# Two layers of cross attention on one core: projections cut from 384 to 320 columns, and two reciprocals written to SBUF

## The chip, the cores and the metric

The kernel runs on one core of a Trainium2 chip. The metric is the device time of one execution in microseconds (us), from three runs. A core has a matrix engine (PE, whose weight loads are listed apart as PEld), a vector engine (DVE), a scalar engine (ACT), a general engine (POOL), and a sync engine (SP), which here does nothing but issue DMAs. Each takes its instructions in the order of its own queue and waits on semaphores of the others.

## The reference

Two attention layers follow one another on `x` (16 samples, 256 queries, 320 channels) with a context of 16 x 256 tokens x 512 channels. Each layer has 20 heads of 16 channels. Cut to its core, layer 0 is:

```python
text, ip = ctx[:, :77], ctx[:, 77:]
q, k, v = hs @ Wq, text @ Wk, text @ Wv            # 320 columns each
text_out = softmax(q_h k_h^T * scale) v_h           # per head
text_probs = softmax(q k^T * scale)                 # over all 320 channels
sem = (text_probs @ text) @ ip^T * scale
ip_out = softmax(q_h (ip @ Wk_ip)_h^T * scale + 0.5 * sem) * mask @ (ip @ Wv_ip)_h
out = (text_out + ip_out) @ Wout + bout + hs
```

Layer 1 has 252 text tokens and 4 image tokens; its `sem` is a cosine between the attended text of a head and the image tokens. All numbers are 32-bit floats, and the result has to be close to a 32-bit one.

## The kernel before, in words

**High and low parts.** A matrix product is made on PE from operands that are split into a high part, which PE takes without loss, and a low part, the rest. `halves(hi, lo, src)` makes them: ACT copies `src` into `hi` (L147), DVE or POOL subtracts (L148). A full product is high x high + high x low + low x high, that is three matmuls for each 128 rows of the contraction (`prod`, L205).

**Tiles of columns.** Channels of q and k stand as (d, h), 16 x 24 with 4 heads of padding, so 384 columns, three tiles m = 0, 1, 2 of 128 (`CP = 384`, `HP = 24`). The output weights and the residual are padded to 384 by repeating the last 64 of the 320 columns. So 64 of the 384 columns, a sixth, carry nothing that is needed. The places:

- `keys0` and `keys_first` (layer 0, a pair of samples at a time) and `keys1` (layer 1, a sample at a time): for each m, 12 matmuls `prod` of 4 row tiles x 3 terms. Layer 0 does it twice, with 192 columns for the text keys and 360 for the image keys; layer 1 with 252. `keys_out` sends high, high, low to the DRAM buffer `kd`.
- `project` (L542): for each m, 8 matmuls of 256 columns. `queries` uses it with `wq` (L550, L551 make the high and low parts `q`, and three DMAs write them to the DRAM buffer `qd`); `finish` uses it with `wo`, and DVE adds bias and residual (L768).
- `semantic0` (L588) multiplies all three tiles of q with all three of the text keys `kb`, 192 columns of the two parts side by side.

**Stacks and slots.** The heads' operands are read back from `qd` and `kd` in another layout, four heads of a group at a time, into a ring of `qs` and `ks` (`stacks0`, `stacks1`, four slots ahead of use: `LEAD = 4`). There are 80 slots in each layer, five to a sample. A slot of layer 0 makes scores (L666), their maxima (DVE L667, L668), transposes the maxima on PE (L674), sends them into `qs` by four small DMAs of the ACT queue, makes the turned scores (L690), their exponentials (ACT L693), a product with the image factor on POOL (L696) and the sums over values (L723). A slot of layer 1 does the like (L814, L816, L834, L808, L828, L868) and the norm of the attended text (L846, L847, L856, L857, L878).

**Order.** PE's order is written out by the program (`slot0`, `slot1`, and tasks with due times in slots, `task(...)`, which `fill` steps through between the parts of a slot). During the first slots (`begin`) all engines follow the program. After that only PE's queue is pinned; the queues of DVE, ACT, POOL and SP are ordered by the compiler's scheduler. Every DMA is issued from SP (L82), but for the maxima's, which ACT issues (L678, L838).

**PSUM.** Eight banks: scores two, T two, P one, X three. All projections, keys, semantics and norms rotate through the three X banks. `settle0` and `settle1` normalize a slot's result: DVE transposes the bank P into `nt` (L734, L913), writes the reciprocals back into that bank (L737, L738, L922) and multiplies by them (L740, L923).

Of the kernel before, what the change touches and what calls it, by code (L numbers as in the profile page):

```python
# [8 lines left out]
F32 = mybir.dt.float32  # L9
# [7 lines left out]
B = 16  # L17
S = 256
# [15 lines left out]
XROW = 48  # L34

# [13 lines left out]
def xattn2(  # L49
# [47 lines left out]
    words, slots = {"ctb": 1024, "cta": 1024, "raw": 512, "rawc": 512, "kb": 1152, "si": 256, "sp": 128, "wC": 2 * 4 * (H * D + NIP), "mt": S, "mx": 2, "tmp": (NG + 1) * 48, "kst": 4 * S, "rs": 2 * S, "P": 4 * S}, {}  # L97
# [21 lines left out]
    kd = [dram.tile([B // 2, 3, CP, 2, S], F32, name="kd0"), dram.tile([B, 3, CP, 1, S], F32, name="kd1")]  # L119
# [25 lines left out]
    def halves(hi, lo, src, eng=nc.vector, loaded=False):  # L145
        order = queued if loaded else lambda inst: inst
        order(nc.scalar.copy(hi, src))  # L147
        order(eng.tensor_sub(lo, src, f(hi)))  # L148
# [21 lines left out]
    def weights(w_d, tag, half=None, wait=0, raw="raw"):  # L170

        rows, n = w_d.shape
        kt = rows // 128
        w = buf(tag, [128, 2, kt, n], FR)
        yield from in_turn([(w_d[k * 128 : (k + 1) * 128], w[:, 0, k], w[:, 1, k]) for k in range(kt)], wait, raw)
        if half is not None:
            nc.vector.tensor_scalar_mul(w[:, 1, 2], f(w[:, 1, 2]), half)
        return lambda s, k, m=slice(None): w[:, s, k, m]

    def weights_by_column(w_d, wait=0, raw="raw"):  # L180
# [4 lines left out]
        return lambda s, k, m: parts[m.start // 128][:, s, k]  # L185

# [21 lines left out]

    def context(b, n, wait=0):
# [9 lines left out]
        if n == 2:  # L219
# [7 lines left out]
    wkt = buf("wA", [128, 2, 4, CP], FR)  # L227
    wk0 = lambda s, k, m=slice(None): wkt[:, s, k, m]
    wqt = buf("wE", [128, 2, 3, CP], FR)
    wkit = [buf("wB", [128, 2, 4, 128], FR, bufs=SIZES["WB"]) for m in range(3)]  # L230
    wki0 = lambda s, k, m: wkit[m.start // 128][:, s, k]
    rows = lambda w, k: w[k * 128 : (k + 1) * 128]
# [3 lines left out]
            (*ctx0[k], ("rawc", "raw")[k // 2]), (rows(wk0_d, k), wkt[:, 0, k], wkt[:, 1, k], "P"))],  # L236
# [4 lines left out]
    wki_src = wki0_d.rearrange("(k p) n -> p k n", p=128)  # L241
    all_halves(
        [(rows(wq0_d, k), wqt[:, 0, k], wqt[:, 1, k], ("rawc", "raw")[k // 2]) for k in range(3)]
        + [(wki_src[:, :, m * 128 : (m + 1) * 128], w[:, 0], w[:, 1], "P") for m, w in enumerate(wkit)],
        RINGS,
    )
    nc.vector.tensor_scalar_mul(wqt[:, 1, 2], f(wqt[:, 1, 2]), tmask[:, 3:4])
# [7 lines left out]
    wq, wo = [lambda s, k, m=slice(None): wqt[:, s, k, m]], []  # L255
# [27 lines left out]
    hsn = const_tile([128, 3, 8, 2, 16], "hsn")  # L283

# [4 lines left out]
    def keys_out(d, m, kst, b=slice(None)):  # L289

        rows = slice(m * 128, (m + 1) * 128)
        for r, s in ((slice(0, 2), 0), (slice(2, 3), 1)):
            src = kst[:, s, b].rearrange("p b t -> p (b t)").unsqueeze(1)
            dma(d[r, rows, b].rearrange("r p b t -> p r (b t)"), src.to_broadcast([128, r.stop - r.start, src.shape[2]]))
# [3 lines left out]
    def keys0(c):  # L298
# [7 lines left out]
        kt = kts[c] = buf("kb", [128, 3, 2, 2, 96], FR, name="kt")  # L306
        for m in range(3):
            ms = slice(m * 128, (m + 1) * 128)
            kst = buf("kst", [128, 2, 2, S], FR, bufs=SIZES["KST"])
            for w, lo, hi, a, z in ((wk0, 0, 96, 0, T0), (wki0, T0 - 1, S, T0, S)):  # L310
                kp = bank()[:, : 2 * (hi - lo)].rearrange("p (b t) -> p b t", b=2)
                prod(kp, lambda s, k: w(s, k, ms), lambda s, k: ct(s, k)[:, :, lo:hi], 4)
                halves(kst[:, 0, :, a:z], kst[:, 1, :, a:z], kp[:, :, a - lo : z - lo])
                if a:
                    keys_out(kd[0][c], m, kst)
                else:
                    nc.gpsimd.tensor_copy(kt[:, m, :, :, :T0], f(kst[:, :, :, :T0]))
                yield

    def keys_first():  # L320
# [4 lines left out]
        kt = kts[0] = buf("kb", [128, 3, 2, 2, 96], FR, name="kt")  # L325
        nc.gpsimd.memset(f(kt), 0.0)
        for w, lo, hi, a, z in ((wk0, 0, 96, 0, T0), (wki0, T0 - 1, S, T0, S)):
            for m in range(3):
                ms = slice(m * 128, (m + 1) * 128)
                kp = bank()[:, : 2 * (hi - lo)].rearrange("p (b t) -> p b t", b=2)  # L330
                prod(kp, lambda s, k: w(s, k, ms), lambda s, k: ct(s, k)[:, :, lo:hi], 4)
                halves(kst[m][:, 0, :, a:z], kst[m][:, 1, :, a:z], kp[:, :, a - lo : z - lo])
                if a:
                    keys_out(kd[0][0], m, kst[m], slice(0, 1))
                else:
                    nc.gpsimd.tensor_copy(kt[:, m, :, :, :T0], f(kst[m][:, :, :, :T0]))
# [64 lines left out]
    def weights7():  # L401
        cip = w1["cip"]
        wki1 = yield from weights_by_column(wki1_d, 0.3, "rawc")
        for m in range(3):
            kp = bank()[:, :BI]
            prod(kp, lambda s, k: wki1(s, k, slice(m * 128, m * 128 + 128)), lambda s, k: cip[:, s, k], 4)
            halves(kip[:, 0, m], kip[:, 1, m], kp)
            yield
# [50 lines left out]
    def keys1(b):  # L459
        ct = ct1[b] = yield from context(b, 1, 0.3)  # L460
        for m in range(3):
            ms = slice(m * 128, (m + 1) * 128)
            kst = buf("kst", [128, 2, 2, S], FR, bufs=SIZES["KST"]).rearrange("p s b t -> p (s b t)")
            kst = kst[:, : 2 * S].rearrange("p (s b t) -> p s b t", s=2, b=1)
            kp = bank()[:, :T1]
            prod(kp, lambda s, k: w1["k"](s, k, ms), lambda s, k: ct(s, k)[:, :T1], 4)
            halves(kst[:, 0, 0, :T1], kst[:, 1, 0, :T1], kp)
            nc.gpsimd.tensor_copy(kst[:, :, 0, T1:], f(kip[:, :, m, 4 * b : 4 * b + 4]))
# [12 lines left out]
    def tokens1(b):  # L481
# [18 lines left out]
        for t, lo in ((0, 0), (1, DUP)):  # L500
# [11 lines left out]
            else:  # L512
# [7 lines left out]
                )  # L520
                yield
# [706 lines left out]
```

## Time and profile before

| | before |
|---|---|
| median of 3 runs | 1559.4 us (1552.63 to 1561.22) |
| the profiled execution | 1561.03 us, span 1559.3 us |
| PE busy | 1472.0 us (94%), 13050 matmuls in the records |
| DVE busy | 1162.4 us (75%) |
| ACT busy | 843.9 us (54%) |
| POOL busy | 1191.4 us (76%) |
| chain that ended last | PE 73%, DMA 12%, DVE 6% |
| DMA | 245.84 MB, 158 GB/s in the mean |

Busy times are the union of an engine's instructions. Matmuls are pipelined and their ends are modelled, so what one matmul costs is read from the starts of a run of equal ones, not from its listed duration. "Granted clock" is the share of full speed that PE was given. The chain is followed backwards from the last instruction; what is not on it had slack.

### The profile page before, as it was taken

Reading aid. Unit: us, or ns where it says so; the run is one execution under the profiler, and the core shown is the slowest. Engines: PE = TensorE matmul, PEld = TensorE weight load, DVE = VectorE, ACT = ScalarE, POOL = GpSimd, SP = SyncE. Lnnn points to the kernel's source line nnn. Section 1 sums busy time; section 2 is a strip of 40 time slices with the busy share of each in tenths; the row PEclk is TensorE's granted clock in tenths of the full one; section 3 lists DMA queues with packets and bytes.
Section 4 is the critical chain, followed back from the end, with each engine's and each line's share of the span. In section 5 each row is a group of like instructions: output and inputs, shape, how many; then the busy total and the mean of one; then the engine's idle time right before and its main releaser. Section 6 shows DMA issues by size and latency. Waiting matters only on the chain.

```text
span 1559.3 us, 36275 instructions
## 1 busy us (share of the span) xinstructions
PE 1472.0 (94%) x13050; PEld 1205.3 (77%) x13050; DVE 1162.4 (75%) x2538; ACT 843.9 (54%) x1858; POOL 1191.4 (76%) x1245
## 2 busy tenths in 40 slices
PE   6899999989998999879999999999999999999996
PEld 6788887878787878757777777777787777877764
DVE  5467676767676777877877887788777877788785
ACT  5345454545454544545655665566655665566561
POOL 3269696878786876778687787878887897779785
PEclk9899999999999999999999999999999999999998
DMA  6777677677767676766544344434444344434411
GB/s 222 207 218 209 193 192 217 192 210 197 216 172 228 168 214 189 212 175 184 138 136 132 98 144 138 133 119 121 140 124 132 106 147 127 139 99 122 128 31 37
DMA packets 256111, 245.84 MB, mean 158 GB/s; under 512 B 37354, under 2 KB 239820, under 8 KB 255916
## 3 DMA queue, kind: packets, MB, share of 16 engines
q1 hardware_dynamic: 253724, 242.22, 52.8%
q8 instruction: 104, 1.70, 0.5%
q10 hardware_dynamic: 2208, 1.30, 0.3%
q14 instruction: 75, 0.61, 0.1%
HBM read 118.24 MB, written 89.69 MB: 133 GB/s over the span
## 4 chain that ended last, share of the span: by engine, by line
PE 73%; DMA 12%; DVE 6%; issue 2%; POOL 2%; SPq 1%; ACT 1%; ACTq 0%; POOLq 0%; DVEq 0%
PE X L856 16%; PE X L205 15%; PE X L542 9%; PE P L868 5%; PE P L723 5%; PE P L878 4%; PE S L666 4%; PE T L808 3%; PE S L814 3%; PE T L690 3%; DMA kd<-kst 2%; DMA qs<-mt 2%; PE X L504 2%; DMA qs<-qd 2%; DMA qd<-q 2%
## 5 line engine op out<-in xcount | busy, mean ns | idle before, releaser
L696 POOL TENSOR_TENSOR P<-P,rs 128x512 f32<-128x512 f32 x320 | 412.3, 1310 | 149.5 <-ACT P L693 149.2
L847 POOL TENSOR_TENSOR wt<-P,ctb 128x512 f32<-128x512 f32 x320 | 410.7, 1304 | 81.2 <-ACT ctb L846 80.9
L856 PE MATMUL X<-ctb,gm 128*128 128x512 f32 x1120 | 303.7, 401 | 0.2 <-DVE wt L857 0.2
L693 ACT ACTIVATE P<-T 128x512 f32<-128x512 f32 x320 | 175.4, 594 | 206.4 <-PE T L690 117.8
L857 DVE TENSOR_TENSOR wt<-X,wt 128x512 f32<-128x512 f32 x320 | 215.1, 681 | 24.0 <-PE X L856 20.5
L828 ACT ACTIVATE P<-T 128x512 f32<-128x512 f32 x320 | 173.4, 594 | 103.5 <-PE T L808 101.5
L856 PEld LDWEIGHTS X<-ctb,gm 128*128 128x128 f32 x1120 | 196.2, 189 | 30.9 <-DVE wt L857 0.4
L846 ACT ACTIVATE ctb<-P 128x512 fp32r<-128x512 f32 x320 | 187.7, 627 | 19.2 <-PE X L856 15.1
L816 DVE TENSOR_REDUCE mn<-S 128x4 fp32r<-128x1008 f32 x160 | 191.5, 1197 | 0.0
L668 DVE TENSOR_REDUCE mn<-S 128x4 fp32r<-128x716 f32 x160 | 142.6, 891 | 0.0
L666 PE MATMUL S<-ks,qs 125*128 125x256 f32 x640 | 118.2, 309 | 18.2 <-DMA ks<-kd 7.0
L666 PEld LDWEIGHTS S<-ks,qs 125*128 125x128 f32 x640 | 89.1, 196 | 54.6 <-issue 35.3
L723 PE MATMUL P<-P,vr 128*32 128x256 f32 x1920 | 126.3, 393 | 1.2 <-DVE mx L595 1.2
L542 PE MATMUL X<-ho,wF 128*128 128x256 f32 x768 | 110.5, 288 | 8.4 <-ACT ho L531 4.3
L542 PE MATMUL X<-hq,wE 128*128 128x256 f32 x768 | 111.5, 290 | 7.0 <-ACT hq L531 4.3
L690 PE MATMUL T<-qs,ks 127*128 127x256 f32 x640 | 109.7, 293 | 6.7 <-DMA qs<-mt 3.6
L542 PEld LDWEIGHTS X<-ho,wF 128*128 128x128 f32 x768 | 103.5, 194 | 14.9 <-ACT ho L531 5.3
L542 PEld LDWEIGHTS X<-hq,wE 128*128 128x128 f32 x768 | 105.0, 195 | 12.0 <-ACT hq L531 4.7
L944 POOL TENSOR_TENSOR r<-u,rs 128x40 f32<-128x40 f32 (+2 forms) x17 | 108.7, 6393 | 4.8 <-DVE u L941 4.8
L205 PE MATMUL X<-cta,wA 128*128 128x252 f32 (+1 forms) x720 | 101.1, 288 | 6.3 <-ACT wA L147 5.3
L205 PEld LDWEIGHTS X<-cta,wA 128*128 128x128 f32 x720 | 96.3, 197 | 10.1 <-ACT wA L147 5.5
L690 PEld LDWEIGHTS T<-qs,ks 127*128 127x128 f32 x640 | 92.3, 198 | 9.8 <-DMA qs<-mt 5.2
(203 smaller groups left out, 2794.6 us busy)
## 6 DMA issues: line engine op xcount, KB each, us to landing
qd<-q SPq DMA_DIRECT2D x96, 384.0 KB
qs<-tph SPq DMA_DIRECT2D x64, 308.0 KB
kd<-kst SPq DMA_DIRECT2D x73, 256.0 KB
rawc<-in_cT_dram SPq DMA_DIRECT2D x60, 256.0 KB
qs<-qd SPq DMA_DIRECT2D x80, 192.0 KB
ks<-kd SPq DMA_DIRECT2D x80, 192.0 KB
ks<-kd SPq DMA_DIRECT2D x160, 96.0 KB
qs<-qd SPq DMA_DIRECT2D x160, 96.0 KB
```

What stands on the lines that cost most here:

```text
L205: last = mm(out, lhs(a, k), rhs(b, k), start=i == 0, stop=i == len(terms) - 1)
L542: mm(pp, w(s, k, slice(m * 128, (m + 1) * 128)), a[:, t], start=i == 0, stop=i == len(terms) - 1)
L666: mm(sp[:, h], Q[: XROW + T0, h, t * 128 : (t + 1) * 128], K[: XROW + T0, h], start=True, stop=True)
L690: mm(st[p][:, j], K[:KS0, 2 * p + j, t * 128 : (t + 1) * 128], Q[:KS0, 2 * p + j], start=True, stop=True)
L693: exp = anchor(nc.scalar.activation(pt, st[p], AF.Exp, scale=SCALE))
L696: anchor(nc.gpsimd.tensor_mul(pt, pt, rs[:, t : t + 1].to_broadcast([128, 2, S])))
L723: mm(pv[32 * s : 32 * s + 32, o : o + S], v[:, vt, h : h + 32], P[k, s // 2][:, t, s % 2], start=vt < 2, stop=vt != 1,)
L816: anchor(nc.vector.tensor_reduce(maxes[k + 2][:, t], sp[:, :, :T1], axis=AX.X, op=ALU.max))
L846: nc.scalar.activation(R[k, u][:, t], P[k, u][:, t], AF.Copy, scale=0.5)
L847: anchor(nc.gpsimd.tensor_sub(W[k, u][:, t], P[k, u][:, t], f(R[k, u][:, t])))
L856: mm(yp, gm[:, gb], R[k, u][:, kt], start=i == 0, stop=i == len(blocks[n]) - 1)
L857: nc.vector.tensor_mul(W[k, u][:, n], yp, W[k, u][:, n])
```

## The change

- Weights of the projections are stored as 320 high columns, then 64 low ones of the last 64 columns, then the other 256 low ones (`rounded`, `columns`). The third tile's weights are so 64 high and 64 low columns side by side. For m = 2 `prod_m` issues two matmuls for a row tile (high and low part of the moving operand) in place of three; `project` issues five in place of eight. m = 0 and 1 stay as they are.
- The result of m = 2 has its two parts on partitions 0 to 63 and 64 to 127. `evacuate` adds them: ACT copies the upper half to SBUF, DVE adds the lower one, and `halves` splits the sum. In `finish` DVE adds the upper half after bias and residual, and in layer 0 ACT copies the 64 rows to the upper half of `y`.
- `qd` and `kd` have 320 rows in place of 384 (`CH`). `queries` issues five DMAs in place of three: three of tiles 0 and 1, ahead of the matmuls of tile 2, and two of tile 2. Heads of a group are stacked in order, so `stacks1` reads two neighbouring heads.
- The text keys are made of 78 columns for a sample in place of 96, in `keys` and `semantic0`.
- `settle0` and `settle1` write their reciprocals to a new SBUF buffer `rz`.
- Layer 1's image key weights come by rows (four tiles) in place of by columns (three). A weight tile now takes one ACT copy and two or three DVE subtractions in place of one.
- `keys1` waits for the step `grams` of the sample before, not for the end of its `tokens1`; one due time of `t1`, one of `c1` and the list of `w7` move a little.

The core of the diff:

```diff
+    def rounded(w, heads=True):
+        hi, last, lo = w[:, :CH], w[:, CH : CH + 64], w[:, CH + 64 :]
+        if not heads:
+            return hi, [(lo[:, :256], slice(0, 256)), (last, slice(256, CH))]
+        view = lambda t: t.rearrange("p (d h) -> p d h", h=H)
+        return view(hi), [(view(lo), slice(0, 13)), (last[:, :4], 12, slice(16, H)), (view(last[:, 4:]), slice(13, D))]
+    def columns(s, m):
+        at = m * 128 if not s else CH + 64 + m * 128
+        return slice(at, at + 128)
+    def prod_m(out, w, m, rhs, kt):
+        if m < 2:
+            prod(out, lambda s, k: w(s, k, m), rhs, kt)
+            return out
+        for i in range(2 * kt):
+            mm(out, w(0, i // 2, 2), rhs(i % 2, i // 2), start=i == 0, stop=i == 2 * kt - 1)
+        return out
+    def evacuate(hi, lo, out, m):
+        if m < 2:
+            return halves(hi, lo, out)
+        hi, lo = hi[:64], lo[:64]
+        both = buf("both", list(hi.shape), bufs=2)
+        nc.scalar.copy(both, out[64:])
+        nc.vector.tensor_add(both, out[:64], both)
+        halves(hi, lo, both)
...
-            for w, lo, hi, a, z in ((wk0, 0, 96, 0, T0), (wki0, T0 - 1, S, T0, S)):
+            for w, lo, hi, a, z in ((wk0, 0, T0 + 1, 0, T0), (wki0, T0 - 1, S, T0, S)):
...
-            for i, (s, k, t) in enumerate(terms):
-                mm(pp, w(s, k, slice(m * 128, (m + 1) * 128)), a[:, t], start=i == 0, stop=i == len(terms) - 1)
+            if m < 2:
+                for i, (s, k, t) in enumerate(terms):
+                    mm(pp, w(s, k, m), a[:, t], start=i == 0, stop=i == len(terms) - 1)
+            else:
+                for t in (0, 3, 1, 4, 2):
+                    mm(pp, w(0, t % 3, 2), a[:, t], start=t == 0, stop=t == 2)
...
-        yield from project(l, wq[l], a, evac)
-        qd = dram.tile([3, CP, S], F32, tag=f"qd{l}", name=f"qd{l}", bufs=2)
+        qd = dram.tile([3, CH, S], F32, tag=f"qd{l}", name=f"qd{l}", bufs=2)
+        steps = project(l, wq[l], a, evac)
+        for m in range(2):
+            next(steps)
+            yield
         for r, s in ((0, 0), (1, 1), (2, 0)):
-            dma(qd[r].rearrange("(m p) t -> p m t", p=128), qh[:, s])
+            dma(qd[r, :256].rearrange("(m p) t -> p m t", p=128), qh[:, s, :2])
+        next(steps)
+        for r, s in ((slice(0, 3, 2), 0), (slice(1, 2), 1)):
+            to = qd[r, 256:].rearrange("r p t -> p r t")
+            dma(to, qh[:64, s, 2].unsqueeze(1).to_broadcast(list(to.shape)))
+        yield
...
-        rz = pv[:, :16].rearrange("p (a f) -> p a f", a=2)
+        rz = buf("rz", [128, 2, 8], bufs=2)
...
             nc.vector.scalar_tensor_tensor(
-                y[:, m], pp, bo[:, l, m : m + 1], resid[:, m], op0=ALU.add, op1=ALU.add
+                y[:n, m], pp[:n], bo[:n, l, m : m + 1], resid[:n, m], op0=ALU.add, op1=ALU.add
             )
+            if m == 2:
+                nc.vector.tensor_add(y[:64, 2], y[:64, 2], pp[64:])
+                if l == 0:
+                    nc.scalar.copy(y[64:, 2], y[:64, 2])
...
-        rz = pv[:, S : S + 8]
+        rz = buf("rz", [128, 2, 8], bufs=2)[:, 0]
...
-        task(("k1", b), shifted(n, -7, -6.67, -6.33, -5.67, -5, -4.67), lambda b=b: keys1(b), ("w2",), *([("t1", b - 1)] if b else []), *([("w4", 1)] if b > 2 else []))
-        task(("t1", b), shifted(n, -3.67, -3, -2.67, -2.33, -2), lambda b=b: tokens1(b), ("k1", b), ("w3", b % 2))
+        task(("k1", b), shifted(n, -7, -6.67, -6.33, -5.67, -5, -4.67), lambda b=b: keys1(b), ("w2",), *([("grams", b - 1)] if b else []), *([("w4", 1)] if b > 2 else []))
+        task(("t1", b), shifted(n, -3.67, -3, -2.67, -2.33, -1.67), lambda b=b: tokens1(b), ("k1", b), ("w3", b % 2))
```

135 lines of the change are left out of this document (75 added, 60 removed).

## The prediction, made before the result was known

> **What bounds the kernel now.** I read the page's busy times, then busy times by stage, then the chain of waits by stage, since the two layers turn out to have different limits. The stages are the start, the slots of layer 0, the passage, the slots of layer 1, the end (columns: PE, PEld, DVE, ACT, POOL busy, granted clock, DMA share, GB/s; the first two rows are one place inside layer 0).
>
> ```profile
> PE 1472.0 (94%) x13050; PEld 1205.3 (77%) x13050; DVE 1162.4 (75%) x2538; ACT 843.9 (54%) x1858; POOL 1191.4 (76%) x1245
> ```
> ```profile
> 156.00:162.50 6.50, 3.48 (x24) 3.29 (x22) 2.85 (x7) 2.27 (x5) 2.92 (x3) 0.92 0.70 176
> 162.50:169.00 6.50, 6.50 (x57) 5.65 (x57) 3.56 (x7) 3.42 (x7) 3.32 (x5) 0.82 0.28 104
> 0.00:100.00 100.00, 80.68 (x541) 71.96 (x541) 54.31 (x123) 43.73 (x101) 37.05 (x47) 0.90 0.74 223
> 100.00:700.00 600.00, 553.37 (x5110) 473.62 (x5108) 436.27 (x989) 297.60 (x685) 470.01 (x455) 0.97 0.69 198
> 700.00:770.00 70.00, 65.72 (x587) 52.66 (x588) 51.39 (x113) 39.25 (x86) 51.69 (x61) 0.98 0.60 166
> 770.00:1490.00 720.00, 716.68 (x6375) 567.62 (x6374) 575.79 (x1221) 436.67 (x939) 582.54 (x629) 1.00 0.41 126
> 1490.00:1560.00 70.00, 55.53 (x446) 39.46 (x444) 44.60 (x98) 26.68 (x50) 50.15 (x55) 0.91 0.11 35
> ```
>
> In layer 1 PE is idle for 720 − 716.68 = 3.3 us in 720; POOL and DVE stand at 81% and 80%. PE alone sets the time there. In layer 0 PE is idle for 47 us in 600. The chain by line (100 to 700 us, then 770 to 1490) and the longest waits of PE in layer 0 say what it waits for.
>
> ```profile
> by line: PE X L205 16.6%; PE P L723 10.4%; PE S L666 8.8%; PE X L542 7.7%; PE T L690 6.7%; DMA kd<-kst 6.3%; DMA qd<-q 4.3%; DMA qs<-qd 3.8%; DMA ks<-kd 3.7%; DMA qs<-mt 3.4%; issue 2.8%; DMA qs<-tph 2.8%; SPq L82 2.3%; DVE mn L668 2.2%; PO
> ```
> ```profile
> by line: PE X L856 31.2%; PE X L205 14.5%; PE X L542 10.1%; PE P L868 9.6%; PE P L878 8.3%; PE T L808 6.6%; PE S L814 6.3%; PE X L504 3.4%; PE X L981 2.4%; PE X L834 2.0%; issue 0.8%; DVE wt L857 0.6%; DMA qs<-mt 0.6%; SPq L82 0.5%; DMA qs<
> ```
> ```profile
> PE S L666 <- DMA ks<-kd: 7.0, 3, 3.0
> PE X L674 <- DVE mn L668: 6.9, 9, 1.5
> PE X L607 <- DVE sp L603: 4.7, 2, 2.4
> PE S L666 <- DMA qs<-qd: 4.3, 3, 2.5
> ```
>
> Layer 1's chain is matmuls nearly throughout. Layer 0's has some 24% in the transfers that carry keys, queries and maxima out and back (6.3 + 4.3 + 3.8 + 3.7 + 3.4 + 2.8): while they are on the chain, PE works at something with slack. So a matmul that is removed counts in full in layer 1, and in layer 0 only where it lies on the chain.
>
> **Matmuls removed.** Their price is the distance of starts in a run of equal ones (start, modelled duration, count).
>
> ```profile
> 1004.33 1.12 PE L542 MATMUL X<-ho,wF 128*128 128x256 f32 x8
> 1005.29 0.86 PE L856 MATMUL X<-ctb,gm 128*128 128x512 f32 x3
> ...
> 1031.17 1.60 PE L205 MATMUL X<-cta,wA 128*128 128x252 f32 x12
> 1032.61 1.78 PE L856 MATMUL X<-ctb,gm 128*128 128x512 f32 x7
> ```
> ```profile
> 235.53 0.81 PE L205 MATMUL X<-cta,wA 128*128 128x192 f32 x6
> 236.18 0.83 PE L205 MATMUL X<-ctb,wA 128*128 128x192 f32 x6
> ...
> 239.43 1.14 PE L205 MATMUL X<-cta,wB 128*128 128x360 f32 x6
> 240.41 1.15 PE L205 MATMUL X<-ctb,wB 128*128 128x360 f32 x6
> ```
> ```profile
> 601.13 1.45 PE L205 MATMUL X<-kst,wB 128*128 128x64 f32 x12
> 602.41 0.29 PE L674 MATMUL X<-ident_r,mn 128*8 128x128 f32 x2
> ```
> ```profile
> L542 PE MATMUL X<-ho,wF 128*128 128x256 f32 x768 | 110.5, 288 | 8.4 <-ACT ho L531 4.3
> L542 PE MATMUL X<-hq,wE 128*128 128x256 f32 x768 | 111.5, 290 | 7.0 <-ACT hq L531 4.3
> ```
>
> 256 columns: 0.96/8 = 0.120 us. 252: 1.44/12 = 0.120. 192: 0.65/6 = 0.108. 360: 0.98/6 = 0.163. 64 columns: 1.28/12 = 0.107.
> - `project`: 1536 matmuls of L542 are 192 tiles of 8; 64 are third tiles, each loses 3: 192 x 0.120 = 23.0 us, half in each layer.
> - `keys1`: 16 x 4 x 0.120 = 7.7 us, layer 1.
> - Layer 0's keys, 8 pairs x 4: 32 x 0.108 + 32 x 0.163 = 3.5 + 5.2 = 8.7 us. `weights7`: 4 x 0.107 = 0.4 us.
>
> Layer 0: 11.5 + 8.7 = 20.2 us. Layer 1: 11.5 + 7.7 + 0.4 = 19.6 us. Together 39.8 us.
>
> **Matmuls made narrower.** 8 x (12 + 12 + 8) text-key matmuls and 192 semantic ones go from 192 to 156 columns. The rows for 64 and 192 columns cost the same (0.107 and 0.108 us), so I take nothing. By slope between 192 and 360 columns (0.055/168 us a column), 36 columns would be 0.012 us, 448 x 0.012 = 5.3 us: the other end, for the range. [...]
>
> **What layer 0 keeps of its 20.2 us.** L542 is on the chain for 7.7% of 600 = 46 us there. It is busy for 93.45:
>
> ```profile
> 100.00:700.00 600.00, 93.45 (x664) 86.38 (x664) 0.97 0.69 198
> ```
>
> Half of it is on the chain, so I take half: 10 us. Ends: 20.2, and 0 if the transfers hold the stage where it is. The new `qd` and `kd` write a sixth less, 64 + 192 KB a sample, 4.2 MB of 198 GB/s x 600 us = 119 MB, 3.5%; of the 24% of chain in transfers (146 us) that would be 5 us if they went by bytes. I take none and keep it for the low end.
>
> **Longer eviction of the third tile.** These rows give the prices; the last four bound the reciprocals.
>
> ```profile
> L550 ACT CAST q<-X 128x256 fp32r<-128x256 f32 x96 | 35.9, 373 | 60.0 <-PE X L542 45.6 <-PE X L856 10.7 <-issue 2.9
> L551 DVE TENSOR_TENSOR q<-X,q 128x256 fp32r<-128x256 f32 x96 | 39.5, 416 | 22.7 <-ACT q L550 22.4
> ...
> L737 DVE RECIPROCAL P<-nt 128x16 f32<-128x16 f32 x80 | 19.9, 249 | 0.0
> L922 DVE RECIPROCAL P<-nt 128x8 f32<-128x8 f32 x80 | 16.6, 208 | 2.5
> L960 DVE RECIPROCAL z<-z 128x40 f32<-128x40 f32 x15 | 6.0, 402 | 0.5
> L602 DVE RECIPROCAL mx<-mx 128x1 f32<-128x1 f32 x32 | 4.9, 154 | 11.6 <-ACT sp L599 11.3
> ```
>
> A sample of layer 1 gains three DVE additions (queries, keys, output) of about 0.416 and two ACT copies of 0.373: 1.25 and 0.75 us. DVE goes to (575.8 + 15 x 1.25)/(720 − 18) = 85%, POOL, unchanged, to 582.5/702 = 83%, ACT to 64%. All stay below PE, so I cost them nothing; if DVE took PE's cover away, a third of the additions in front of PE (16 x 0.42) would be 7 us. The X bank is free after a copy and an addition, as before after a copy and a subtraction; only in `finish` 0.42 us later, with two more banks in the ring. In layer 0 the additions are the same kind and in the same shade, besides one 64-row ACT copy before the output's DMA, which a later slot reads.
>
> **Reciprocals.** 154, 208, 249, 402 ns for 1 and 40 elements in SBUF and 8 and 16 to PSUM lie on one line, so writing to SBUF saves nothing that I can see: 0, at most some 0.03 us each for 240 instructions, 7 us of DVE, not of PE. The P bank is released earlier; no wait for it stands among PE's.
>
> **DMAs.** Queries issue five for three, on SP's in-order queue and ahead of the stacks of later slots. Per sample:
>
> ```profile
> 217.64 2.42 SPq L82 DMA_DIRECT2D qd<-q  x3
> ```
>
> 0.81 us each now; with two thirds of the rows 0.54, and the small ones a third and a sixth of one: 3 x 0.54 + 0.54 + 0.27 = 2.4 us, no change. The first three wait for tile 1 and not for tile 2, the last two for two more instructions (0.79 us, plus up to one reduction of the queue); stacks that use them come slots later. Nothing taken. Two neighbouring heads in `stacks1` make fewer, larger pieces where the DMAs are at 0.41: nothing. Weights: one or two DVE pieces more for 11 tiles at the start, at least 0.154 each, 3 to 6 us beside a DVE busy 54 of 100: nothing, bound +4. The moved dues and `grams` remove a short wait before L522 and move no work of PE between slots: nothing. At the end three matmuls less against one DVE addition (0.42): nothing.
>
> **Sum.** −19.6 − 10 = −29.6 us, 1.9%. The profiled execution took 1561.03 us (1.7 around its span), 1.6 above the median of the three runs; against the median, 1559.4 − 29.6 = 1530 us. Within 0.5% (1551.6 to 1567.2) I call no change.
>
> **Rivals.**
> - *All of it counts.* Layer 0's idle time shrinks along because its transfers hang on PE's earlier work. 39.8 to 45 us with the narrower columns: 1514 to 1520. For: three lines of layer 0's matmuls lead the chain. Against: the 24% of transfers. 0.2.
> - *DVE or transfers take over.* Layer 0 gives nothing and layer 1 loses the 7 us: 1540 to 1547. For: DVE at 85%, in-order, with 1.2 us reductions that hold an eviction back. Against: PE's waits for DVE in layer 1 are now below 3.3 us in all. 0.2.
> - *More idle time, lower clock.* In layer 0 a gap of 3.0 us (L666 waiting for `ks<-kd`, the row above) is followed by a clock of 0.92 and 0.82: 0.08 x 3.48 + 0.18 x 6.5 = 1.4 us lost, 4.4 with the gap. Less PE work between the same transfers makes gaps longer. One new such gap for each of the 7 later pairs is 31 us: layer 0 is 10 us worse than now in spite of its 10, layer 1 keeps its 20: 1559.4 − 29.6 + 31 = 1561. Against: a gap of 3 us is rare now (three waits of that kind in all). 0.07. [...]
> - *Slower: the third tile blocks SP.* The two late DMAs of `qd` wait for a chain longer by two instructions, 0.79 us, and each may stand behind a 0.6 us exponential or a 0.9 us reduction: up to 2.3 us, in which SP issues no stack. At 16 samples that is 37 us, and if layer 0 has no gain otherwise: 1559.4 − 19.6 + 37 = 1577. It decides from 27/16 = 1.7 us a sample on. For: `qd<-q` has 4.3% of layer 0's chain. Against: PE waits 4.3 us in all for `qs<-qd`, and stacks are issued four slots ahead. 0.08.
> - The change can't fail to remove its matmuls: the count is in the program.
>
> **How the numbers follow.** The forecast, 1522 to 1540, has 0.45. Faster: 0.45 + 0.2 + 0.18 of the second rival = 0.83. Same: its rest, the clock's and a part of the fourth, 0.10. Slower: 0.07. The range reaches from all gains with the transfers' 5 us and a little of the reciprocals' (1559.4 − 45 − 5 − 4 = 1505) to DVE's case with the start's 4 and a gap or two (1554); it leaves the two last rivals out.
>
> **What would show it.** 324 matmuls fewer, L542's and the keys' groups short by those counts; in layer 1 PE idle for still some 5 us in 700, five samples shorter by 5 x 1.2 us; the spacing of 156 columns at 0.107 us; in layer 0 transfers with a larger share of the chain than 24% and PE busy below 92%. Wrong would be: PE in layer 1 waiting for DVE or ACT at L542 and `keys1`, new waits of L666 for `qs<-qd`, or a clock below 0.97 in layer 0.

## The result, and the profile after

The changed kernel takes 1608.3 us (median of four runs; 1606.3 to 1609.1) against 1560.3 us before: 1.0309 times as long, 95% interval 1.0263 to 1.0355. It is 48 us slower. I had forecast 1530 us, faster.

The engines' rows and the chain by engine, from the page of after:

```profile
PE 1464.6 (91%) x12726; PEld 1173.0 (73%) x12726; DVE 1351.9 (84%) x2687; ACT 877.0 (55%) x1941; POOL 1213.1 (76%) x1246
```
```profile
PE 54%; DVE 22%; POOL 9%; DMA 6%; issue 4%; ACT 1%; SPq 1%; ACTq 0%; DVEq 0%; POOLq 0%
```

PE has its 324 matmuls less. DVE has 189 us more (1351.9 − 1162.4) and goes from 6% of the chain to 22%. The stages of after (start, inside layer 0, inside layer 1; columns as in the prediction):

```profile
0.00:100.00 100.00, 73.04 (x463) 66.08 (x464) 57.57 (x146) 42.51 (x101) 37.83 (x46) 0.91 0.65 195
100.00:720.00 620.00, 553.29 (x4953) 460.67 (x4952) 548.75 (x1045) 313.52 (x721) 475.54 (x448) 0.95 0.64 182
800.00:1530.00 730.00, 709.06 (x6266) 548.53 (x6259) 627.48 (x1265) 449.12 (x969) 589.70 (x631) 1.00 0.41 117
```

In layer 0 DVE stands at 548.75/620 = 89% (73% before) and the granted clock at 0.95 (0.97). In layer 1 PE is idle for 21 us of 730 (3.3 of 720 before). PE's longest waits of after, from 100 to 700 us and then from 800 to 1500:

```profile
PE X L238 <- DVE tph L672: 12.3, 6, 2.1
PE X L594 <- DVE both L258: 9.1, 6, 1.5
PE X L650 <- DVE q L153: 7.6, 7, 1.9
PE X L597 <- DVE both L258: 6.5, 6, 1.1
```
```profile
PE X L922 <- DVE wt L923: 16.2, 13, 1.4
PE X L594 <- POOL hq L583: 2.4, 12, 0.2
```

All but the last are waits for DVE; before, the longest in layer 0 was one for a DMA. Which DVE work grew? The view of one line lists shortest/median/longest duration in ns. Before, the three products with the reciprocals:

```profile
L738 DVE TENSOR_TENSOR P<-P,mk x80: 145/168/175, 77.3 to 742.3; 128x8 f32<-128x8 f32 x80
L740 DVE TENSOR_TENSOR tmp<-nt,P x80: 403/420/423, 77.5 to 742.5; 128x256 f32<-128x256 f32 x80
L923 DVE TENSOR_TENSOR hsn<-nt,P x80: 260/286/290, 747.1 to 1530.4; 128x128 f32<-128x128 f32 x80
```

After, the same three:

```profile
L799 DVE TENSOR_TENSOR rz<-rz,mk x80: 96/798/1299, 83.9 to 772.8; 128x8 f32<-128x8 f32 x80
L801 DVE TENSOR_TENSOR tmp<-nt,rz x80: 404/1410/1524, 84.7 to 773.1; 128x256 f32<-128x256 f32 x80
L989 DVE TENSOR_TENSOR hsn<-nt,rz x80: 270/447/1420, 780.9 to 1572.8; 128x128 f32<-128x128 f32 x80
```

A product of 8 elements takes up to 1.3 us where it took 0.17. By groups, the three go from 13.2 + 33.3 + 22.6 to 56.1 + 79.9 + 55.1 us: 122 of DVE's 189. In the kernel before, one factor of each stood in PSUM (P); now both stand in SBUF. The split of the third tile shows the same thing, since its sum `both` is in SBUF (groups of after, then mean ns of one behind the comma):

```profile
L153 DVE TENSOR_TENSOR q<-X,q 128x256 fp32r<-128x256 f32 x64 | 25.8, 411 | 8.3 <-ACT q L150 8.1
L153 DVE TENSOR_TENSOR q<-both,q 64x256 fp32r<-64x256 f32 x32 | 22.6, 707 | 2.4 <-ACT q L150 2.4
```

What holds such an instruction can be seen in the timeline. In after, around 303 us, POOL and DVE do this (start, duration; two POOL products follow one another in the first line):

```profile
302.92 2.55 POOL L757 TENSOR_TENSOR P<-P,rs 128x512 f32<-128x512 f32 x2
```
```profile
303.62 0.62 DVE L799 TENSOR_TENSOR rz<-rz,mk 128x8 f32<-128x8 f32 x1
304.27 1.48 DVE L801 TENSOR_TENSOR tmp<-nt,rz 128x256 f32<-128x256 f32 x1
```

POOL's first product ends at some 302.92 + 2.55/2 = 304.20, and L799 at 303.62 + 0.62 = 304.24. POOL's second ends at 305.47, and L801 at 305.75. From the single records: of the 80 L799, 78 start while a POOL instruction runs, and the middle 80% of these end 0.020 to 0.026 us behind that instruction's end, however long that is; L801 ends a median of 0.281 us behind it (60 of 80), L989 0.147 (65 of 80). Those that start while POOL is idle take 0.152, 0.410 and 0.282 us, no more than before the change. The distance behind POOL's end grows with the elements, 0.022 us in the median for 8, 0.147 for 128 and 0.281 for 256, some 1 ns for each: the work on the elements lies behind that end. So these products, with both inputs in SBUF, stood still until the running POOL instruction was over.

The lengths of the two layers come from DVE's transposes, of which each slot has one (first to last start). Before:

```profile
L734 DVE STREAM_TRANSPOSE nt<-P x80: 664/717/718, 74.7 to 740.0; 128x512 f32<-128x512 f32 x80
L913 DVE STREAM_TRANSPOSE nt<-P x81: 399/450/451, 746.4 to 1537.6; 128x256 f32<-128x256 f32 x81
```

After:

```profile
L795 DVE STREAM_TRANSPOSE nt<-P x80: 669/717/719, 81.5 to 770.5; 128x512 f32<-128x512 f32 x80
L979 DVE STREAM_TRANSPOSE nt<-P x81: 398/450/451, 780.0 to 1583.8; 128x256 f32<-128x256 f32 x81
```

Start +6.8, layer 0 665.3 to 689.0 (+23.7), the passage between the layers +3.1, layer 1 791.2 to 803.8 (+12.6). Such lengths are from one execution. The runs of the kernel before, made side by side, differ by up to 13 us among themselves, and its profiled execution (1561.0 us) is one of the longer ones, so I use the lengths to place a difference and the ratios to size it.

### The profile page after: what moved, and what is told of

Same layout as the page of the kernel before. It is cut to its first block, busy times and chain, and to the rows that moved or that the text cites. A ratio compares the mean times of both kernels' runs of the same rounds, so it can differ in the third digit from the quotient of the medians.

```text
span 1604.5 us, 35927 instructions
## 1 busy us (share of the span) xinstructions
PE 1464.6 (91%) x12726; PEld 1173.0 (73%) x12726; DVE 1351.9 (84%) x2687; ACT 877.0 (55%) x1941; POOL 1213.1 (76%) x1246
## 4 chain that ended last, share of the span: by engine, by line
PE 54%; DVE 22%; POOL 9%; DMA 6%; issue 4%; ACT 1%; SPq 1%; ACTq 0%; DVEq 0%; POOLq 0%
PE X L922 12%; PE X L238 12%; POOL wt L913 6%; PE X L594 5%; PE P L784 5%; PE P L934 4%; DVE mn L729 3%; PE P L944 3%; DMA ks<-M 2%; PE S L880 2%; PE S L727 2%; PE T L874 2%; DVE tmp L801 2%; PE T L751 2%; DVE nt L795 2%
## 5 line engine op out<-in xcount | busy, mean ns | idle before, releaser
L757 POOL TENSOR_TENSOR P<-P,rs 128x512 f32<-128x512 f32 x320 | 416.8, 1325 | 134.4 <-ACT P L754 134.3
L913 POOL TENSOR_TENSOR wt<-P,ctb 128x512 f32<-128x512 f32 x320 | 416.8, 1327 | 81.9 <-ACT ctb L912 79.2
L922 PE MATMUL X<-ctb,gm 128*128 128x512 f32 x1120 | 306.4, 403 | 16.4 <-DVE wt L923 16.2
L922 PEld LDWEIGHTS X<-ctb,gm 128*128 128x128 f32 x1120 | 196.1, 189 | 50.3 <-DVE wt L923 19.2
L912 ACT ACTIVATE ctb<-P 128x512 fp32r<-128x512 f32 x320 | 187.2, 627 | 56.1 <-PE X L922 52.1
L784 PE MATMUL P<-P,vr 128*32 128x256 f32 x1920 | 136.2, 419 | 1.5 <-POOL P L757 1.5
L795 DVE STREAM_TRANSPOSE nt<-P 128x512 f32<-128x512 f32 x80 | 56.8, 710 | 45.9 <-PE P L784 45.7
L784 PEld LDWEIGHTS P<-P,vr 128*32 128x32 f32 x1920 | 58.3, 118 | 48.8 <-issue 14.1
L594 PE MATMUL X<-hq,wE 128*128 128x256 f32 x512 | 79.8, 296 | 12.1 <-ACT hq L582 6.9
L728 DVE TENSOR_REDUCE mn<-S 128x4 fp32r<-128x308 f32 x160 | 74.0, 462 | 19.2 <-PE S L727 19.1
L934 PE MATMUL P<-P,v1t 128*32 128x256 f32 x1280 | 86.4, 388 | 0.0
L594 PE MATMUL X<-ho,wF 128*128 128x256 f32 x512 | 75.1, 291 | 11.1 <-DVE both L258 9.1
```

Of the source, the lines that this page charges most:

```text
L594: mm(pp, w(s, k, m), a[:, t], start=i == 0, stop=i == len(terms) - 1)
L757: anchor(nc.gpsimd.tensor_mul(pt, pt, rs[:, t : t + 1].to_broadcast([128, 2, S])))
L784: mm(pv[32 * s : 32 * s + 32, o : o + S], v[:, vt, h : h + 32], P[k, s // 2][:, t, s % 2], start=vt < 2, stop=vt != 1,)
L912: nc.scalar.activation(R[k, u][:, t], P[k, u][:, t], AF.Copy, scale=0.5)
L913: anchor(nc.gpsimd.tensor_sub(W[k, u][:, t], P[k, u][:, t], f(R[k, u][:, t])))
L922: mm(yp, gm[:, gb], R[k, u][:, kt], start=i == 0, stop=i == len(blocks[n]) - 1)
```

## The experiments

A ratio is the time against the kernel before, run beside it (some 1555 us in the median), with the 95% interval in brackets; a kernel with a single run has no ratio.

### Reciprocals: out of after, into before, and with POOL's work taken away

One edit in three places. First, after with the reciprocals back in PSUM:

```diff
-        rz = buf("rz", [128, 2, 8], bufs=2)
+        rz = pv[:, :16].rearrange("p (a f) -> p a f", a=2)
...
-        rz = buf("rz", [128, 2, 8], bufs=2)[:, 0]
+        rz = pv[:, S : S + 8]
```

> The changed kernel with both reciprocals back in the PSUM bank, all else as changed. Theory A (the SBUF buffer rz makes DVE's products of nt and rz two-SBUF-input instructions, which wait for POOL's): the products at 128x8, 128x256 and 128x128 fall from 0.70, 1.00 and 0.69 us to the 0.17, 0.42 and 0.28 of the kernel before, DVE busy from 1352 to about 1230 us, and the time to 1525 to 1545, below the kernel before. Theory B (the longer eviction of the third tile makes the loss): stays at 1590 or more.

1581.7 us, ratio 1.0178 (1.0138 to 1.0219). The three products fell as theory A said, to means of 0.165, 0.413 and 0.281 us, and DVE to 1239.6 us. The time fell too, but stayed 37 us above the upper end of theory A's range and 8 below theory B's bound: both were wrong on it. Theory A had counted on the gain of the matmuls, which is looked at further below. The transposes:

```profile
L795 DVE STREAM_TRANSPOSE nt<-P x80: 665/717/719, 80.3 to 761.2; 128x512 f32<-128x512 f32 x80
L979 DVE STREAM_TRANSPOSE nt<-P x81: 386/449/451, 768.8 to 1557.7; 128x256 f32<-128x256 f32 x81
```

Layer 1, 788.9 us, is as short as before the change; layer 0, 680.9 us, still is not. Second, the kernel before with only these lines the other way round:

> The kernel before with only the two reciprocals written to SBUF. Theory A: the three products take 0.7, 1.0 and 0.7 us, DVE busy about 1162 + 122 = 1285 us, and the time rises by 30 to 70 us to 1590 to 1630. Theory B: no change, 1555 to 1565.

1595.1 us, ratio 1.0245 (1.0188 to 1.0301), with the columns, the matmuls and the transfers as they were, and inside theory A's range. By groups the three products take 49.6 + 82.7 + 47.3 us, 110 us more than before (DVE's whole busy time grows by 101). Its transposes:

```profile
L734 DVE STREAM_TRANSPOSE nt<-P x80: 664/716/718, 73.5 to 762.4; 128x512 f32<-128x512 f32 x80
L913 DVE STREAM_TRANSPOSE nt<-P x81: 399/450/451, 769.9 to 1573.5; 128x256 f32<-128x256 f32 x81
```

Layer 0 is 688.9 us and layer 1 803.6, the lengths of after. Two lines of the diff are enough to make both layers as slow as the whole change does. That the lengths are so nearly equal is chance in part: after has fewer matmuls and longer evictions besides, and without the two lines its layer 0 was still 680.9 us. Third, after with POOL's product in layer 0 not issued:

```diff
-            anchor(nc.gpsimd.tensor_mul(pt, pt, rs[:, t : t + 1].to_broadcast([128, 2, S])))
```

> The changed kernel without layer 0's product of the exponentials with the image factor on POOL (left out, so the values are not weighted by it). Theory A: in layer 0 the products with rz fall to about 0.17 and 0.42 us, as POOL is nearly idle there; in layer 1 the product stays at 0.69. Theory C (an instruction with both inputs in SBUF is simply slow, whatever POOL does): 0.70 and 1.00 us stay.

1535.3 us in the one run. Layer 0's products of 8 and 256 elements and layer 1's of 128, by line:

```profile
L798 DVE TENSOR_TENSOR rz<-rz,mk x80: 145/166/1210, 81.0 to 701.2; 128x8 f32<-128x8 f32 x80
L800 DVE TENSOR_TENSOR tmp<-nt,rz x80: 407/424/1501, 81.2 to 701.9; 128x256 f32<-128x256 f32 x80
L988 DVE TENSOR_TENSOR hsn<-nt,rz x80: 266/449/1420, 710.2 to 1503.0; 128x128 f32<-128x128 f32 x80
```

Without POOL's product the first two are back at medians of 166 and 424 ns with their operands still in SBUF, but for those few that meet other work of POOL (it is still busy for 119 of the 620 us); in layer 1, where POOL works as ever, the third stays as it was in after. The time itself says less, because the step was also work of a slot. So the cause of the longer products is shown: the SBUF operands by themselves did not slow these products (166 and 424 ns), POOL's running instruction is what they waited for (798 and 1410 ns in after). That the two lines cost time, 38 us of 1555, the kernel before with them shows.

### The sum of the third tile in PSUM

After with the reciprocals in PSUM, and the sum written back to the X bank:

```diff
-        nc.vector.tensor_add(both, out[:64], both)
-        halves(hi, lo, both)
+        nc.vector.tensor_add(out[:64], out[:64], both)
+        halves(hi, lo, out[:64])
```

> As the one with reciprocals in PSUM, and the sum of the third tile's two parts is written to PSUM too, so that the subtraction that follows has only one input in SBUF. Theory A: the subtractions of the third tile fall from 0.71 (256 columns) and 0.72 (252) to 0.41, 17 us of DVE, and the time is 0 to 8 us below that of the reciprocals alone. Theory B has nothing to gain here: the eviction has as many steps.

1572.2 us, ratio 1.0127 (1.0080 to 1.0173): some 0.005 below the run without this edit, though the intervals overlap. The split of q falls from 0.68 to 0.41 us, DVE from 1239.6 to 1225.3 us. Its transposes:

```profile
L795 DVE STREAM_TRANSPOSE nt<-P x80: 665/717/719, 79.7 to 744.9; 128x512 f32<-128x512 f32 x80
L979 DVE STREAM_TRANSPOSE nt<-P x81: 384/449/452, 755.5 to 1547.0; 128x256 f32<-128x256 f32 x81
```

Both layers, 665.2 and 791.5 us, are what they were before the change. That answers what the slowdown of the layers was, and asks the next question: 324 matmuls are gone, and neither layer is a microsecond shorter. All further kernels start from this one or from the kernel before.

### What it is not

**The pieces of the weights.** One subtraction and one ACT copy for a weight tile, in place of two or three subtractions.

> As the one with reciprocals and sum in PSUM; besides, a weight tile's low parts are made by one DVE subtraction again (all 320 side by side), and ACT copies the last 64 of them next to the high ones. If the pieces of the weights, which are two-SBUF-input instructions that wait for POOL, hold the last samples of layer 0 and the passage back (176 us for four samples became 183, and 6 us of passage 11), this gains 5 to 12 us against it. If the start and the passage are slow because the third tile's eviction has more steps in series, 0 to 3 us.

1573.7 us, ratio 1.0107 (1.0064 to 1.0150): no difference that can be told.

**POOL's power.** POOL takes 6.8 us for the inverse square root of a sample of layer 1. I suspected that it keeps the split queries back. Twice the power was replaced by a logarithm and an exponential on ACT, in the kernel above and in before:

```diff
-        pool.tensor_tensor(r, u, w1["mhalf"].rearrange("p (f s) -> p f s", f=NG)[:, gs], op=ALU.pow)
+        nc.scalar.activation(r, u, AF.Ln)
+        nc.scalar.activation(r, r, AF.Exp, scale=-0.5)
```

> As the one with reciprocals and sum in PSUM; the inverse square root of the image part is made on ACT as exp(-0.5 ln u) in place of POOL's power of 6.8 us. Theory D (in layer 1 POOL's full stretch of 21 us from the power to the queries' low parts sets a sample's time, and PE waits behind it for what the removed matmuls gave): the sample's period falls from 50.8 to about 49.5 us, 15 to 25 us in all. Theory E (DVE sets the period): it stays at 50.8.

> The kernel before with the same inverse square root on ACT. Theory D: PE is busy all through layer 1 there, so its period stays within 0.4 us of 50.5, and the time within 6 us of before; the difference between this and the one with the changed columns is then the 1.2 us a sample of the removed matmuls.

1635.8 us (1.0510, 1.0478 to 1.0542) and 1575.1 us (1.0119, 1.0083 to 1.0156). Both slower, and they tell little: 34 table loads of 1.283 us came in, 17 for each of the two functions. So the power was then replaced by a plain product on POOL:

> As the one with reciprocals and sum in PSUM, with POOL's power of 6.8 us in layer 1 left out (a product of 0.26 us stands in its place, so the weights of the image tokens are not normalized by it). No table is loaded, unlike in the two kernels with the square root on ACT. Theory D (POOL's stretch after the power holds the gain): the sample's period falls from 50.8 to 49.0 to 49.8 us. Theory E (DVE's burst between the maxima and the next products does): 50.4 to 50.8.

> The kernel before with the same power left out. PE is busy for all of layer 1 there, so by D and E alike the period stays at 50.2 to 50.6 us, the 1.2 us of the third tile's matmuls above what theory D gives for the changed one.

1583.4 and 1559.4 us, one run each. A sample of layer 1 (five transposes), in the mean of the middle twelve, took 52.3 us where it had taken 50.7, and 51.2 where the kernel before takes 50.7. Less POOL work did not help; why a sample even got longer stays open. Splitting the queries two slots earlier, out of the way of that work, by their due times:

```diff
-        task(("o1", b), shifted(n, -7.67, -7, -6.67, -5.33, -4.33, -4), ...
+        task(("o1", b), shifted(n, -9.67, -8.9, -6.67, -5.33, -4.33, -4), ...
```

> As the one with reciprocals and sum in PSUM, with layer 1's query input loaded and split about two slots earlier, so that POOL makes its low parts right behind the power and not at the end of its full stretch. Theory D: PE no longer waits for them, the period falls by 0.5 to 1.2 us and the time by 7 to 18 us. Theory E: no change within 3 us.

1590.5 us, ratio 1.0216 (1.0181 to 1.0250): slower, where one theory had a gain and the other no change. Theory D fell; why it is slower stays open.

**DVE's last step of the output's split**, which has two SBUF operands (1.1 us each):

> As the one with reciprocals and sum in PSUM, without DVE's last step of the split before the output projection (the low part of the third tile of its input is left out), 1.1 us a sample with two SBUF inputs. Theory E: the period of layer 1 falls by 0.7 to 1.2 us, to below 50.1. Theory D: it stays at 50.5 to 50.8.

1559.0 us in one run; a sample of layer 1 took 50.5 us for 50.8 in the median. The direction is theory E's, the size less than half of what it asked for, so the run decides between neither.

### The matmuls' price, and the eviction's

Four kernels separate what was taken from PE and what was put on the way out of PSUM. The kernel before with nothing but the 324 matmuls left out:

```diff
-        terms = [(k, a, b) for k in range(kt) for a, b in ((0, 0), (0, 1), (1, 0))]
+        terms = [(k, a, b) for k in range(kt) for a, b in ((0, 0), (0, 1), (1, 0))[: 3 if m < 2 else 2]]
...
+            ours = [x for x in terms if m < 2 or x[0] == 0]
```

> The kernel before, with nothing changed but that the third tile's matmuls with the weights' low part are not issued (8 in place of 12 for the keys, 5 in place of 8 for queries and outputs); the result lacks that part in the third tile. This is the price of the removed matmuls alone, with before's evictions, columns, transfers and reciprocals. My forecast's own step: 19.6 us in layer 1 and 10 in layer 0, so 1527 to 1535, ratio 0.98 to 0.985. Theory N: within 5 us of before, ratio 0.997 to 1.0. In between: the share of the forecast that the matmuls were worth.

1551.1 us, ratio 0.9963 (0.9944 to 0.9982): 0.0037 x 1555 = 6 us, where I had counted 29.6. The transposes, and PE's longest waits from 100 to 700 us:

```profile
L735 DVE STREAM_TRANSPOSE nt<-P x80: 671/717/718, 72.8 to 738.2; 128x512 f32<-128x512 f32 x80
L914 DVE STREAM_TRANSPOSE nt<-P x81: 399/450/452, 745.6 to 1525.1; 128x256 f32<-128x256 f32 x81
```
```profile
PE X L543 <- DVE ho L532: 10.0, 5, 2.0
PE S L667 <- DMA qs<-qd: 8.9, 6, 2.5
PE X L675 <- DVE mn L669: 5.6, 5, 2.2
PE T L691 <- DVE tmp L741: 5.4, 5, 3.3
```

Layer 1 gets shorter by 11.7 us (779.5 against 791.2; a sample 49.77 against 50.67 in the mean of the middle twelve). Layer 0 gets nothing (665.4 against 665.3): PE is busy 6 us less in the 600 (547.27 against 553.37) and waits for it, for `qs<-qd` 8.9 us in place of 4.3, and for DVE up to 10 us at one line. Next, the kernel with everything in PSUM, with the matmuls put back in number (the extra ones write the bank first and are overwritten):

```diff
+        for i in range(kt):
+            mm(out, w(0, i, 2), rhs(0, i), start=i == 0, stop=i == kt - 1)
         for i in range(2 * kt):
```

> The kernel with reciprocals and sum in PSUM, with the third tile's matmuls brought back to before's number (12 in place of 8 for the keys, 8 in place of 5 for the rest): the extra ones write the same bank first and are overwritten. Long evictions, no matmul saved. Theory M: the matmuls saved come back, 20 to 30 us above 1572, about 1597, ratio 1.03. Theory N: 1572 to 1578, ratio 1.013 to 1.017.

1584.0 us, ratio 1.0178 (1.0139 to 1.0218), some 8 us up, with intervals that overlap; it lies between the two theories, nearer to N. In layer 1 the same price comes out again, 802.8 against 791.5, +11.3:

```profile
L799 DVE STREAM_TRANSPOSE nt<-P x80: 665/717/719, 80.3 to 749.8; 128x512 f32<-128x512 f32 x80
L983 DVE STREAM_TRANSPOSE nt<-P x81: 391/449/451, 758.1 to 1560.9; 128x256 f32<-128x256 f32 x81
```

Then the same kernel without the copy and the addition:

```diff
-        both = buf("both", list(hi.shape), bufs=2)
-        nc.scalar.copy(both, out[64:])
-        nc.vector.tensor_add(out[:64], out[:64], both)
-        halves(hi, lo, out[:64])
+        halves(hi[:64], lo[:64], out[:64])
...
-                nc.vector.tensor_add(y[:64, 2], y[:64, 2], pp[64:])
```

> The kernel with reciprocals and sum in PSUM (1572 us, ratio 1.013), and in it the third tile's lower half dropped at the eviction: its 64 rows are split from PSUM with no copy of the low part and no addition, as a tile of before is, and layer 1's last step adds nothing. The product with the weights' low part is computed and left out of the result. So 324 matmuls are gone and the evictions are no longer than before's. Theory M (the matmuls are worth what I forecast, and the longer eviction takes it away again): 20 to 30 us below 1572, about 1545, ratio 0.99. Theory N (a sample's time is not set by the number of matmuls, and the eviction costs little): 1562 to 1572, ratio 1.005 to 1.013.

1563.7 us, ratio 1.0043 (1.0019 to 1.0067), clear of the 1.0127 with the addition: 0.0084 x 1555 = 13 us for the eviction. Theory M's 1545 did not come, since the matmuls are not worth what I had forecast. And with the addition made shorter, ACT's copy left out and the low half added last:

```diff
+        halves(hi, lo, out[:64])
+        nc.vector.tensor_add(lo, f(lo), out[64:])
```

> The kernel with reciprocals and sum in PSUM, with one step fewer in the third tile's eviction: ScalarE rounds the upper 64 rows at once, VectorE subtracts as ever and then adds the lower 64 rows from PSUM to the low part, so ScalarE's copy of the lower rows goes and no instruction has two operands in SBUF. Theory M (the eviction's length is the loss): 1555 to 1565, ratio 1.00 to 1.008. Theory N: 1568 to 1573, ratio 1.011 to 1.014.

1588.0 us, ratio 1.0197 (1.0174 to 1.0220): slower, against both theories. Layer 1 is a little shorter (789.7 against 791.5), layer 0 25 us longer (690.4 against 665.2). From 80 to 740 us, with PE's longest waits there:

```profile
80.00:740.00 660.00, 584.43 (x5218) 493.61 (x5217) 490.88 (x1100) 315.30 (x731) 491.74 (x480) 0.93 0.64 184
```
```profile
PE X L733 <- DVE tmp L799: 13.6, 3, 4.5
PE X L595 <- DVE q L257: 12.0, 6, 2.9
PE T L749 <- DVE tmp L799: 11.9, 4, 4.5
```

Waits of up to 4.5 us, and a clock of 0.93 where the longer eviction has 0.97. I can't say why the scheduler's new order of DVE gives such waits; that layer 0's length hangs on that order more than on the amount of work, the run shows.

### The rest: due times and the queries' transfers

The kernel without addition has the matmuls of the one at 0.9963 and stands at 1.0043. With the due times and waits of before:

> The kernel whose third tile is split with no addition (ratio 1.004; the weights' low part stays out of the third tile's result), with the due times and the waits of layer 1's tasks put back to before's (the tokens' last step at -2, the closing's last at 13, the keys behind the whole tokens of the sample before). It has 324 fewer matmuls as the kernel before without them has (0.996), and is 8 to 12 us longer. If the due times are the cause: a sample of layer 1 in 49.8 us in place of 50.35, 1552 to 1557, ratio 0.997 to 1.000. If not: 1560 to 1566.

1560.4 us, ratio 1.0044 (1.0022 to 1.0067): not them, in the whole. In the profiled execution layer 1 did get shorter (783.8 for 787.1 us) and layer 0 longer (668.0 for 663.4). With the queries' rows sent after all three tiles, as before, though in six DMAs for before's three (the lines added):

```diff
+        yield from project(l, wq[l], a, evac)
+        for r, s in ((0, 0), (1, 1), (2, 0)):
+            dma(qd[r, :256].rearrange("(m p) t -> p m t", p=128), qh[:, s, :2])
+            dma(qd[r, 256:], qh[:64, s, 2])
```

> The same kernel without the addition, with the query rows sent as before, after all three tiles are split and row set by row set, in place of the first two tiles' ahead of the third tile's matmuls (due times as in the changed kernel). If the transfers issued between the second and third tile are what keeps the queries' matmuls waiting in layer 1 (0.86 us of a sample, against none in the kernel before without the 324 matmuls): a sample of layer 1 in 49.8 us, 1552 to 1557, ratio 0.997 to 1.000. If not: 1560 to 1568.

1555.4 us, ratio 1.0004 (0.9976 to 1.0032), some 6 us better, with intervals that overlap. But not where I had placed it: layer 1 stays (788.7 us, 50.4 a sample), layer 0 gets shorter, 735.1 − 77.0 = 658.1 us against 663.4. The transposes of layer 0, without this edit and with it:

```profile
L791 DVE STREAM_TRANSPOSE nt<-P x80: 698/717/719, 77.0 to 740.4; 128x512 f32<-128x512 f32 x80
L784 DVE STREAM_TRANSPOSE nt<-P x80: 670/717/719, 77.0 to 735.1; 128x512 f32<-128x512 f32 x80
```

### The sum

| step, undone one after the other | ratio | us of it |
|---|---|---|
| the changed kernel | 1.0309 | |
| reciprocals back in PSUM | 1.0178 | 20 |
| sum of the third tile in PSUM | 1.0127 | 8 |
| no copy and no addition | 1.0043 | 13 |
| queries' rows sent at the end | 1.0004 | 6 |
| before, without the 324 matmuls | 0.9963 | 6 |
| before | 1 | −6 |

The first and the third step stand clear of their intervals; the others are estimates within them. The last but one is what is left between the kernel of the line above it and the kernel before without the matmuls. By the profiled executions that is the start (the first slot settles at 77.0 us against 72.8), the passage (9.0 against 7.4) and layer 1 (788.7 against 779.5), while layer 0 is 7 us shorter; what makes it was not tested. The steps don't simply add: alone in the kernel before the reciprocals cost 38 us, last in after 20.

## Why the prediction was wrong

**"Writing to SBUF saves nothing that I can see: 0."** This is the step that failed, the largest of several. I priced the instruction that writes the reciprocals, and that price held (L798 237 ns, 249 before). What I left out is that three products that read `rz` change their operand with it. They cost 110 us of DVE and 38 us of time when nothing else is changed, and 122 us of DVE in the whole change. The profile before had the sign. These are DVE lines of the kernel before, the first two with no PSUM operand, the last with one (X):

```profile
L532 DVE TENSOR_TENSOR ho<-hT,ho x32: 649/1655/1830, 126.2 to 1549.9; 128x512 fp32r<-128x512 f32 x32
L603 DVE TENSOR_SCALAR sp<-sp,mx x32: 253/532/1429, 28.4 to 650.2; 128x77 f32<-128x77 f32 x32
L591 DVE TENSOR_TENSOR sp<-sp,X x32: 223/230/238, 26.9 to 645.3; 128x77 f32<-128x77 f32 x32
```

A median of 1655 ns over a shortest of 649 on the same shape was a wait inside the instruction. The single records show for what: 25 of the 32 L532 start while a POOL instruction runs and end a median of 0.551 us behind its end, the other seven take 0.651 us in the median; of L603, 22 of the 32 do so and end 0.060 us behind it, the other ten take 0.262. My quoted bounds were means of single-input reciprocals, which show nothing of it.

**"A matmul that is removed counts in full in layer 1": 19.6 us.** 11.7 by the profiled lengths. Spacing and count were right: 10 matmuls fewer in a sample are 1.2 us by my rows, and a sample got 0.9 us shorter. By the starts of the matmuls, the keys (L205) gave their share in full, 0.47 us a sample for four, but the projections 0.35 for six, which I had at 0.72. Three new gaps a sample take the rest, of 0.22 to 0.35 us from one start to the next where others have 0.12; one lies before L522, which waits for DVE's `gm`, and what makes the two between a projection's first and second matmul stays open. PE counts as busy through them, since they are hardly longer than the modelled durations (288 ns in the mean for L542), so PE idle for 3.3 us in 720 could not show how much of that time was work.

**"What layer 0 keeps: I take half, 10 us."** 0. Its end of the bounds was 0, "if the transfers hold the stage"; but the waits above are for DVE more than for transfers, so it was not only the transfers that hold it. In whole executions matmuls alone are worth 6 us, a fifth of the 29.6 forecast. These 24 us that did not come and the 20 + 8 + 13 + 6 + 6 us of the table are nearly all of the 78 us between −29.6 and +48.

**"All stay below PE, so I cost them nothing."** The longer eviction costs 13 us with the sum in PSUM and some 21 with it in SBUF (13 + 8, the 8 within the intervals). DVE's share in layer 1 came out near my 85%, at 627.48/730 = 86%, but by luck: some 55.1 − 22.6 = 32 us of it are L989's waits for POOL, and the kernel with everything in PSUM has 638.62/780 = 82%. A share below PE's was no cover here: the X banks turn through ACT and DVE in their queues' order, and PE waits for the instruction, not for the share. In after it waited 9.1 + 6.5 us for `both` at the projections of layer 0. My own bound, 16 x 0.42 = 7 us, took one addition's own duration, and neither the queue ahead of it nor layer 0.

**Queries' DMAs, "nothing taken".** About 6 us, in layer 0, an estimate within the intervals. **Weights, "nothing, bound +4"**: nothing that can be told. **Moved dues**: nothing that can be told. **Narrower matmuls, nothing**: right. The 156-column rows of after start 0.67/6 = 0.112 us apart, and over all such pairs the median is 0.111 us, as for 192 columns in before:

```profile
236.73 0.83 PE L238 MATMUL X<-cta,wA 128*128 128x156 f32 x6
237.40 0.83 PE L238 MATMUL X<-ctb,wA 128*128 128x156 f32 x6
```

**Rivals.** "DVE or transfers take over" had the place right and the price wrong: it ended at 1547, since it knew of nothing that would make DVE's old instructions longer. "More idle time, lower clock" came in part: the clock is 0.95 in layer 0, but PE's longest waits there (12.3, 9.1, 7.6 and 6.5 us in sum at their lines) are for DVE, not for transfers. The one slower rival, the third tile blocking SP, is not what made the time: neither `qd` nor `qs<-qd` stands among PE's waits of after inside the two layers, though sending the queries' rows early may have cost the 6 us above. Of the signs that I had named for being wrong, a clock below 0.97 in layer 0 came, and PE in layer 1 waiting for DVE, but at L922 (L856 of before), not at the projections and keys that I had named. PE busy below 92% in layer 0, a sign of being right, came too (553.29/620 = 89%), for the wrong reason: the transfers' share of the chain did not grow, DMA went from 12% to 6% of the whole.

## What to carry to other kernels

When an operand moves from PSUM to SBUF, price its readers, not only its writer: list every DVE instruction that then has both inputs in SBUF. Here, beside a POOL busy 76% of the time with products of 1.33 us, their means went from 0.17, 0.42 and 0.28 us to 0.70, 1.00 and 0.69. In a profile, compare shortest, median and longest of one DVE line; in the kernel before the sign of that wait was a spread of 649 to 1830 ns on one shape (L532), as much as one of POOL's products (1.31 us in the mean), and that the long ones ended 0.551 us behind an instruction of POOL told it. And when a matmul is traded for an addition on the way out of PSUM, price the trade with the matmuls alone left out first: here they were worth 6 us and the eviction cost 13.

## What was unexpected of the hardware

- DVE and POOL: an 8-element product ended 0.020 to 0.026 us behind the end of the POOL instruction that ran when it started; 0.15 us without one. With one operand in PSUM, in the kernel before, it was never held (145 to 175 ns, L738).
- Two ACT functions, a logarithm and an exponential in turn, brought one table load of 1.283 us for each, 34 in all.
- A shorter eviction made layer 0 25 us longer, with longer waits of PE for DVE and a granted clock of 0.93 in place of 0.97; its cause stays open.
